# Moving entry 0's stores to ScalarE's queue, ending its projections four steps early, and telling the planner what entry 0 leaves open

## The chip, the cores and the metric

The kernel runs on one core of a Trainium2 chip. A core has five engines that work side by side and wait for each other through semaphores: TensorE (PE in the profile; its weight loads are PEld), VectorE (DVE), ScalarE (ACT), GpSimd (POOL) and SyncE (SP), which here only issues DMAs. Each engine takes its instructions in order; a DMA is issued by an engine's queue and then runs by itself on sixteen DMA engines. The metric is the device time of one execution in microseconds; three executions of the kernel before are known, and one more was profiled.

## The reference

The inputs are `x` of shape (8, 2048, 256) in float32 (eight entries of a batch, 2048 nodes, 256 features) and a 2048 x 2048 0/1 matrix `adj`. Two graph layers follow, each as a residual with a layer norm:

```
layer 0:  v = x W (8 heads of 32);  e_ij = leaky_relu(es_i + ed_j, 0.2) + beta*log(adj_ij + 1e-6), -inf where adj_ij = 0
          x1 = layernorm(x + concat_h(softmax_j(e) v) W_out^T)
layer 1:  e_ij = leaky_relu((x1 W1)_i . (x1 W2)_j, 0.2), -1e12 where adj_ij = 0
          out = layernorm(x1 + relu(softmax_j(e) (x1 W3)))
```

## The kernel before

Everything is float32. Entry 0's layer 0 comes first and alone. Then, for each entry b, layer 1 of entry b runs together with layer 0 of entry b + 1, so that eight stretches of some 300 us follow the first one.

**Layer 0** works in strips. The heads go in four pairs, the 2048 queries in two halves; that makes eight units per entry, with 16 key tiles each: 128 strips. For one strip a tile `mt` (128 keys x 1024 queries, the weighted adjacency, kept in DRAM as `mt_d`) is loaded, VectorE makes two tiles `s` from it (L439 in entry 0, L988 later), and TensorE multiplies them with the values (`val`, L475) and, for some or all strips, with the denominator weights (`den`, L475). In entry 0 every strip has `val` and `den`. From entry 1 on, eleven strips of a unit first get a scaling by ScalarE (L424), and GpSimd sums them (L996) in place of `den`; the last five are direct.

**Entry 0** is written as a loop of 64 steps of two strips. In its first 16 steps it also builds the tiles: `make_m` (L220) loads a block of `adj`, VectorE, ScalarE twice and VectorE again turn it into `m` (L226 to L229), and `make_mt` (L235) transposes `m`, copies it on ScalarE (L241) and stores it to `mt_d` (L242). Between steps it advances the generator `others` (L793), which projects the seven other entries: TensorE's `proj` (L299), ScalarE's copies `v` and `both` (L301, L303), a store of `v` to `v_d` (L824), and at the end of each entry `factors` (the softmax factors `re`, stored by L827) and `queries` (the row `est`, stored to `c_d` by L340). The generator yields 56 times, 1.75 times per two steps, and once more after the loop for the last entry's `queries`.

When a unit ends, `divide` turns its denominator into a factor: a store and reload of `dn` to a narrow tile `rc` (L504), a reciprocal on VectorE and its store to `rec_d` (L508, L509), a load of the broadcast `rb` (L518), and a multiplication `ht` by `rb` on VectorE (L523). With the last unit's multiplication the head outputs of entry 0 are complete, and the projection `y` (L1115) can start.

**Who sets the order.** In entry 0 only TensorE's order is fixed, to the order of the code; the other engines are ordered by the framework. From L847 on every engine follows a written order, which a planner at build time (`Sched`, L660) writes out: it has a list of tasks with costs, dependencies, an extra latency `late`, and slots for the buffers (9 of them in the ring for `s`, 4 for `mt`), and emits at each moment the task that can start first. TensorE chooses between "full" work (`y`, the transposes `tr`, the projections `h`, the scores `e`, `T`, `acc`) and strips: when a strip is ready, it goes first if the strips eaten so far are behind a goal line by more than a few,

```
S.goal = lambda w: NP * 2 * NT * (w + 28.0) / span      # w: us of full work so far, span = 303
```

Each engine's and SP's part of this order starts with what is emitted right after L847: the last `queries`, then the second part of the last `divide` (reciprocal and store to `rec_d`), and then the planner's tasks. Four planner tasks named `tinyd` (L885) carry the rest of that `divide`, the first of them the loads of `rb`; all the `y` wait for the last of them.

Of the kernel before, what the change touches and what calls it, by code (L numbers as in the profile page):

```python
# [18 lines left out]
P = 128  # L19
# [8 lines left out]
def kernel(  # L28
# [26 lines left out]
    nc = tc.nc  # L55
    B, N, D = x.shape
    H, _, DH = w_proj.shape
    NT = N // P
# [5 lines left out]
    NP = H // HP  # L64
    IG = BK // P
# [2 lines left out]
    J2 = NT // 2  # L68
    DIRECT = [[range(NT)] * NP] + [[(11, 12, 13, 14, 15)] * NP] * (B - 1)
    SLOTS = 9  # L70

    const = ctx.enter_context(tc.tile_pool(name="const", bufs=1))
    dram = ctx.enter_context(tc.tile_pool(name="dram", bufs=1, space=DRAM))
# [8 lines left out]
    def mm_tile(name):  # L82
        tag = banks[0]
        banks.append(banks.pop(0))
        return pacc.tile([P, BK], F32, tag=tag, name=name)
# [3 lines left out]
    def pair_tile(name):  # L89
        pairs.append(name)  # L90
        return pacc.tile([P, 2, BK], F32, tag=f"c{len(pairs) % 2}", name=name)

    homes = {"s": [f"s{i}" for i in range(SLOTS)], "h": [f"h{i}" for i in range(4)], "mt": [f"mt{i}" for i in range(4)],
             "row": [f"row{i}" for i in range(4)]}
# [15 lines left out]
    def leave(t):  # L110

        home, at, _ = home_of.pop(id(t))
        homes[home].append(at)
        return at
# [4 lines left out]
    def h_tile(name, shape, tag=None, dtype=F32):  # L119
        return home_tile("h", name, shape, dtype, tag)  # L120
# [54 lines left out]
    def later_weights():  # L175

        nc.sync.dma_start(w3s, w3.rearrange("(k p) d -> p k d", p=P))
        w1t, w2t = (chunk.tile([P, KC, D], F32, tag="pt", name=name, bufs=NB) for name in ("w1t", "w2t"))
        for w, dst in ((w_out, wot), (w1, w1t), (w2, w2t)):
            src = [row_tile("square") for _ in range(KC)]  # L180
            for o in range(KC):
                nc.sync.dma_start(src[o], w[ts(o, P), :])
            yield
            for kc in range(KC):
                t = mm_tile("sq_t")
                for o in range(KC):
                    nc.tensor.transpose(t[:, ts(o, P)], src[o][:, ts(kc, P)], ident)
                nc.scalar.copy(dst[:, kc, :], t[:, 0:D])
        yield
        for dc in range(KC):  # L190
            t = mm_tile("w12p")
            for kc in range(KC):
                nc.tensor.matmul(t[:, 0:D], w1t[:, kc, ts(dc, P)], w2t[:, kc, :], start=(kc == 0), stop=(kc == KC - 1))
            nc.scalar.copy(w12[:, dc, :], t[:, 0:D])
        yield


    mt_d = dram.tile([2 * J2, P, 2, HALF], F32, name="mt_d")
    pen_d = dram.tile([N, N], BF16, name="pen_d")
    c_d = dram.tile([B, H, N], F32, name="c_d")  # L200
    v_d = dram.tile([B, NP, P, NT, HP * DH], F32, name="v_d")
    re_d = dram.tile([B, P, 2, NT, H], F32, name="re_d")
# [3 lines left out]
    def load_x(b, g):  # L206

        xg = wide.tile([P, IG, D], F32, tag="pen", name="xg", bufs=1)
        nc.sync.dma_start(xg, x[b].rearrange("(t p) d -> p t d", p=P)[:, ts(g, IG), :])
        return xg  # L210

    def transpose_x(xg, dst):

        for kc in range(KC):
            t = mm_tile("tr")
            for k in range(IG):
                nc.tensor.transpose(t[:, ts(k, P)], xg[:, k, ts(kc, P)], ident)
            nc.scalar.copy(dst[kc], t)
# [13 lines left out]
    def mt_tile(tag=None):  # L232
        return home_tile("mt", "mt", (P, HALF), F32, tag)

    def make_mt(n, i, m):  # L235

        mt = mt_tile()
        t = pair_tile("mtp").rearrange("p a n -> p (a n)")
        for k in range(NT // 2):
            nc.tensor.transpose(t[:, ts(k, P)], m[:, k, ts(i, P)], ident)  # L240
        nc.scalar.copy(mt, t)  # L241
        nc.sync.dma_start(mt_d[n, :, i], mt)  # L242
        return mt

    def load_mt(n, i, tag=None):
# [4 lines left out]
    def row_tile(name, tag=None):  # L250
        return home_tile("row", name, (P, D), F32, tag)
# [14 lines left out]
    class Gat:  # L266


        def __init__(self, b):
            self.b = b  # L270
            self.ms, self.mts, self.v, self.mv = [], [], {}, None
# [62 lines left out]
        def queries(self):  # L334

            t = mm_tile("est")
            nc.tensor.transpose(t[:, 0:P], self.sums_c.rearrange("p h t -> p (h t)"), ident)
            est = row_tile("est")[:, 0:P]
            nc.scalar.activation(est, t[:, 0:P], AF.Exp, scale=1.0 - ALPHA)
            nc.sync.dma_start(c_d[self.b].rearrange("h (t p) -> (h t) p", p=P), est)  # L340

        def load(self, hp):
            self.v[hp] = chunk.tile([P, NT, HP * DH], F32, tag="v", name="v", bufs=2)
# [294 lines left out]
    class Task:  # L638
# [8 lines left out]
        def ready(self):  # L647
# [9 lines left out]
                t = max(t, at)  # L657
            return t

    class Sched:  # L660


# [130 lines left out]
    def others():  # L793

        order = gats[2:-2] + gats[1:2] + gats[-2:]
        groups = [(gat, g) for gat in order for g in range(NB)]
        xgs, xts, xtiles = [], [], []

        def load(n):
            if n < len(groups):  # L800
                xgs.append(load_x(groups[n][0].b, groups[n][1]))

        def turn(n):
            if n < len(groups):
                xt = h_tile("xt", (P, KC, BK))
                xtiles.append(xt)
                xts.append([xt[:, kc, :] for kc in range(KC)])
                transpose_x(xgs[n], xts[n])
                load(n + 1)

        load(0)
        yield
        turn(0)
        for n, (gat, g) in enumerate(groups):
            if g == 0:
                gat.begin()
            v = chunk.tile([P, NP, IG, HP * DH], F32, tag="v", name="v", bufs=2)
            for k in range(0, IG, 2):
                gat.rows_in(g * IG + k, xts[n], v[:, :, ds(k, 2), :])
                if k == 0:  # L820
                    turn(n + 1)
                else:
                    leave(xtiles[n])
                    nc.sync.dma_start(v_d[gat.b].rearrange("h p t f -> p h t f")[:, :, ts(g, IG), :], v)  # L824
                    if g == NB - 1:
                        gat.factors()
                        nc.sync.dma_start(re_d[gat.b], gat.re)  # L827
                    if g == 0 and n > 0:
                        groups[n - 1][0].queries()
                yield  # L830
        order[-1].queries()
        yield

    projections, weights = others(), later_weights()
    next(projections)
    count = (B - 1) * NT // 2
    for k in range(1, NP * NT + 1):
        g0.step(k - 1)
        if k % 2 == 0:
            for _ in range(k * count // (NP * NT) - (k - 2) * count // (NP * NT)):  # L840
                next(projections)
            if k > NT:
                next(weights, None)
# [1 line left out]


    ctx.enter_context(tc.manual_schedule(engines={e.engine for e in (nc.sync, nc.scalar, nc.vector, nc.gpsimd)}))  # L847
    next(projections)
    S = Sched()
    bank = Banks(["m0", "m1", "den"])  # L850
    for work in later:
        next(work)
# [10 lines left out]
    def pe(where, name, busy, emit, deps=(), hold=None, reader=None, easy=True, seam=False):  # L863
# [8 lines left out]
        if reader:  # L872
            queue, rbusy, remit, rdeps = reader
            r = Task(queue, rbusy, lambda: remit(box["t"]), [task] + list(rdeps), (), [hold])
            task.reader = r
            task.after = lambda: S.q[queue].append(r)
        task.box = box
        getattr(S, where).append(task)
        return task

    pending = []
    last = None
    for work in later:
        for _ in range(4):
            last = S.add("tinyd", 0.3, lambda work=work: next(work, None), [last], late=3.0)  # L885
    pending.append(last)
    later[:] = []

# [7 lines left out]
    def layer0(b):  # L896

        gat, E = gats[b], entries[b]
        E.mult, E.turned = {}, None
        E.re = S.add("v", 0.4, gat.load_factors, late=3.0) if b > 1 else None  # L900
        for hp in range(NP):
            if b > 1 or hp > 0:
                hold = Hold(v_s, NT * 2)
                load = S.add("v", 0.4, lambda hp=hp: gat.load(hp), takes=[hold], late=4.0)
                vs = S.add("vscale", 1.15, lambda hp=hp: gat.scale(hp), [load])
            else:
# [284 lines left out]
    def layer1(b):  # L1191
# [175 lines left out]
        def new(it):  # L1367
            R[it] = {"e": [], "T": [], "pts": [], "ph": [], "a": []}

        queries(0)  # L1370
        new(0)
        for c in range(NB):
            scores(0, c)
        soft(0)
        for it in range(NT):
            more = it + 1 < NT
            if more:
                new(it + 1)
            for c in range(NB):
                turn(it, c)  # L1380
                if more:
                    scores(it + 1, c)
            if more:
                soft(it + 1)
            for h in range(8):
                acc(it, h)
            if it + 2 < NT and (it + 2) % IG == 0:
                queries((it + 2) // IG)
            if it == NT - 3:
                E.near = R[it]["a"][-1]  # L1390
# [15 lines left out]
    for a in range(HP):  # L1406
        u.makes[NT - 1, a].after = lambda a=a: bank.give(u.makes[NT - 1, a].end, f"c{a}")
    span = 303.0
    S.goal = lambda w: NP * 2 * NT * (w + 28.0) / span
    S.run()  # L1410
# [1 line left out]
_INS = ['x', 'adj', 'L0_gnn_W', 'L0_gnn_a_src', 'L0_gnn_a_dst', 'L0_gnn_beta_tilde', 'L0_gnn_W_out',  # L1412
# [27 lines left out]
```

## Time and profile before

| | |
|---|---|
| median of 3 runs (lowest, highest) | 4111.2 us (4104.77, 4113.67) |
| the profiled execution's own time | 4113.88 us |
| its span | 4112.1 us |
| PE, DVE, ACT, POOL busy | 97%, 76%, 71%, 67% of the span |
| granted TensorE clock, mean | 0.993 |
| entry 0 (0 to 460 us): PE, DVE, ACT busy | 427.6, 380.7, 187.7 us |
| 460 to 480 us: PE busy | 3.3 of 20 us |
| 480 to 600 us: PE busy | 108.0 of 120 us |
| 900 to 3600 us: PE busy | 2644.6 of 2700 us |

The span is the profiled execution from its first to its last instruction. A busy time is the time in which an engine had an instruction in it; a matmul that waits for its input in the middle of a group counts as busy in part, so a stretch can be emptier than its PE figure. Windows of the trace give the same figures for any stretch, the list of waits says who ended an engine's idle time, and the chain of waits goes back from the last instruction of a stretch to what released each step.

### The profile page before, as it was taken

The numbers are of one execution on the slowest core, as the hardware profiler recorded it, in microseconds if no ns is written. First come the engines' busy times: TensorE is split into PE (matmuls) and PEld (weight loads), VectorE is DVE, ScalarE is ACT, GpSimd is POOL, SyncE is SP. The second block draws the span as 40 slices with busy tenths as digits, with TensorE's granted clock in tenths as the row PEclk, the third lists the DMA queues.
The fourth block names the chain that finished last, engine by engine and source line by source line (L and its number), as shares of the span: only waits on it lengthen the run. The fifth ranks groups of instructions, "written<-read, shape, count | busy, mean of one in ns | idle before, by whom it ended". The sixth has DMA issues, their size and how long they took to land.

```text
span 4112.1 us, 60541 instructions
## 1 busy us (share of the span) xinstructions
PE 3973.1 (97%) x22704; PEld 2157.4 (52%) x22704; DVE 3144.8 (76%) x3343; ACT 2927.6 (71%) x4164; POOL 2747.1 (67%) x1318
## 2 busy tenths in 40 slices
PE   8999899999999999999999999999999999999999
PEld 5444444555555555545555554555555554555666
DVE  7888678788877888888877888878877888786222
ACT  6522478887777778777877788778877887776554
POOL 0000279878787788888878898878878887885000
PEclk9999999999999999999999999999999999999999
DMA  8899767777656666666665676656665666654111
GB/s 274 287 293 308 249 207 242 230 242 260 200 187 199 215 198 207 200 204 220 208 209 185 198 229 209 213 183 223 224 199 185 215 229 207 191 196 131 63 47 41
DMA packets 346439, 843.65 MB, mean 205 GB/s; under 512 B 49696, under 2 KB 166432, under 8 KB 346144
## 3 DMA queue, kind: packets, MB, share of 16 engines
q1 hardware_dynamic: 346144, 839.77, 62.6%
q8 instruction: 178, 2.92, 0.3%
q14 instruction: 117, 0.96, 0.1%
HBM read 763.76 MB, written 75.37 MB: 204 GB/s over the span
## 4 chain that ended last, share of the span: by engine, by line
PE 59%; ACT 11%; DVE 7%; DMA 5%; issue 3%; POOL 3%; SPq 0%; DVEq 0%; ACTq 0%; POOLq 0%
PE e L1229 18%; PE acc L1324 14%; PE val L475 12%; ACT s L424 6%; DVE s L988 5%; PE den L475 5%; PE T L1304 4%; PE h L1178 3%; DMA mt<-mt_d 2%; POOL sums L996 2%; PE h L1204 2%; DVE p L1275 1%; ACT p L1236 1%; PE y L1115 1%; DMA rc<-dn 1%
## 5 line engine op out<-in xcount | busy, mean ns | idle before, releaser
L996 POOL TENSOR_TENSOR sums<-sums,s 128x1024 f32<-128x1024 f32 x1008 | 2366.8, 2389 | 17.6 <-DVE s L988 15.7
L988 DVE SCALAR_TENSOR_TENSOR s<-c,re,s 128x1024 f32<-128x1024 f32 x1232 | 1513.7, 1274 | 285.8 <-ACT s L424 245.7
L424 ACT ACTIVATE s<-mt,re 128x1024 f32<-128x1024 f32 x1232 | 1350.7, 1147 | 104.0 <-DMA mt<-mt_d 75.3
L475 PE MATMUL val<-s,v 128*32 128x512 f32 x8192 | 1014.8, 598 | 32.3 <-issue 14.6
L1229 PE MATMUL e<-x1t,h 128*128 128x512 f32 x2048 | 981.5, 604 | 24.0 <-ACT p L1236 18.2
L1324 PE MATMUL acc<-h,pts 128*128 128x256 f32 x4096 | 911.9, 381 | 0.7 <-ACT pts L1309 0.7
L1324 PEld LDWEIGHTS acc<-h,pts 128*128 128x128 f32 x4096 | 775.5, 190 | 177.1 <-issue 61.9
L988 DVE SCALAR_TENSOR_TENSOR s<-c,re,mt 128x1024 f32<-128x1024 f32 x560 | 679.3, 1275 | 44.1 <-POOL sums L996 18.5
L475 PEld LDWEIGHTS val<-s,v 128*32 128x32 f32 x8192 | 245.2, 110 | 613.9 <-issue 481.7
L1229 PEld LDWEIGHTS e<-x1t,h 128*128 128x128 f32 x2048 | 352.1, 191 | 378.1 <-issue 280.6
L1275 DVE CUSTOM_DVE_ANT_0 p<-p,pen 128x2048 f32<-128x2048 f32 x128 | 336.3, 2627 | 264.8 <-ACT p L1236 260.2
L1236 ACT ACTIVATE p<-e 128x512 f32<-128x512 f32 x512 | 304.7, 595 | 205.2 <-PE e L1229 198.2
L1276 POOL TENSOR_SCALAR neg<-neg 128x1 f32<-128x1 f32 x128 | 26.6, 208 | 615.9 <-DVE neg L1275 610.1
L475 PE MATMUL den<-s,re 128*32 128x512 f32 x3264 | 437.1, 593 | 0.0
L1281 ACT ACTIVATE p<-p,neg 128x2048 f32<-128x2048 f32 x128 | 256.1, 2001 | 223.4 <-POOL neg L1276 222.4
L1304 PEld LDWEIGHTS T<-ident,p 128*128 128x128 f32 x2048 | 250.1, 141 | 281.4 <-issue 174.4
L996 POOL TENSOR_TENSOR sums<-s 128x1024 f32<-128x1024 f32 x112 | 264.7, 2384 | 181.4 <-DVE s L988 181.3
L439 DVE SCALAR_TENSOR_TENSOR s<-c_in,re,mt 128x1024 f32<-128x1024 f32 x256 | 310.4, 1278 | 38.5 <-DMA mt<-mt_d 30.3
L1304 PE MATMUL T<-ident,p 128*128 128x128 f32 x2048 | 311.3, 276 | 24.3 <-ACT p L1281 13.8
L1309 ACT COPY pts<-T 128x512 f32<-128x512 f32 x512 | 296.6, 583 | 30.6 <-PE T L1304 29.3
L310 POOL PARTITION_ALL_REDUCE top<-top x8 | 7.4, 920 | 410.4 <-DVE top L309 410.4
L475 PEld LDWEIGHTS den<-s,re 128*32 128x32 f32 x3264 | 107.9, 110 | 240.9 <-issue 239.4
(99 smaller groups left out, 2476.2 us busy)
## 6 DMA issues: line engine op xcount, KB each, us to landing
mt<-mt_d SPq DMA_DIRECT2D x992, 512.0 KB
c_in<-c_d SPq DMA_DIRECT2D x64, 1024.0 KB
pen<-pen_d SPq DMA_DIRECT2D x112, 512.0 KB
xg<-in_x_dram SPq DMA_DIRECT2D x60, 512.0 KB
adj_t<-in_adj_dram SPq DMA_DIRECT2D x16, 1024.0 KB
mt_d<-mt SPq DMA_DIRECT2D x32, 512.0 KB
rb<-rec_d SPq DMA_DIRECT2D x128, 128.0 KB
adj_r<-in_adj_dram SPq DMA_DIRECT2D x32, 512.0 KB
```

What stands on the lines that cost most here:

```text
L424: nc.scalar.activation(self.s[jt][:, a], self.mt[jt], AF.Copy, scale=self.gat.re[:, 1, jt, h:h + 1])
L439: nc.vector.scalar_tensor_tensor(s[:, a], self.c[a], self.gat.re[:, 0, jt, h:h + 1], m, ALU.max, ALU.mult)
L475: nc.tensor.matmul(dst[ts(q, DH), :], weights[q % 2], s[:, q % 2, ts(q // 2, BK)], start=start, stop=stop)
L988: nc.vector.scalar_tensor_tensor(u.s[jt][:, a], u.c[a], gat.re[:, 0, jt, h:h + 1], m, ALU.max, ALU.mult)
L996: nc.gpsimd.tensor_tensor(u.sums[:, a], of[:, a], u.s[jt][:, a], ALU.add)
L1229: nc.tensor.matmul(t, box["h"][:, kc, ts(it % IG, P)], gat.x1t[:, kc, ts(c, BK)], start=(kc == 0), stop=(kc == KC - 1))
L1236: nc.scalar.activation(pbox["p"][:, ts(c, BK)], t, AF.Prelu, alpha=ALPHA)
L1275: nc.vector.tensor_tensor_reduce(p, p, r["pen"], 1.0, -FMAX, ALU.subtract, ALU.max, neg)
L1281: nc.scalar.activation(p, p, AF.Exp, bias=r["neg"], accum_out=den)
L1304: nc.tensor.transpose(t[:, ts(k, P)], pbox["p"][:, ts(c * IG + k, P)], ident)
L1309: nc.scalar.copy(pt, t)
L1324: nc.tensor.matmul(r["acc"], r["pts"][g][:, ts(k, P)], gat.h3[:, j, :], start=(j == 0), stop=(j == NT - 1))
```

## The change

The planner's and entry 0's orders change in five places.

1. Four DMA issues of entry 0 and its projections go from SP's queue to ScalarE's: the stores to `mt_d`, `c_d`, `v_d` and `re_d`. All of them store what ScalarE wrote.
2. The 56 yields of the projections are spread over 60 steps and not 64, and the last `queries` comes at step 60 and not after the loop, so it's no longer part of the written order.
3. The planner's clock for TensorE starts at 13.0 and not at 0.
4. The first `tinyd` becomes ready at 18.0 and not at 0, and each of the four has 2.0 and not 3.0 of latency.
5. The lead of 28 in the strips' goal grows with the work: 28 * min(1, (10 + w) / 303).

```diff
+    EARLY = 4
@@ make_mt
-        nc.sync.dma_start(mt_d[n, :, i], mt)
+        nc.scalar.dma_start(mt_d[n, :, i], mt)
@@ Gat.queries
-            nc.sync.dma_start(c_d[self.b].rearrange("h (t p) -> (h t) p", p=P), est)
+            nc.scalar.dma_start(c_d[self.b].rearrange("h (t p) -> (h t) p", p=P), est)
@@ new class
+    class Ready:
+        def __init__(self, end):
+            self.end, self.eng, self.late, self.name = end, None, 0.0, "ready"
@@ others
-                    nc.sync.dma_start(v_d[gat.b].rearrange("h p t f -> p h t f")[:, :, ts(g, IG), :], v)
+                    nc.scalar.dma_start(v_d[gat.b].rearrange("h p t f -> p h t f")[:, :, ts(g, IG), :], v)
                     if g == NB - 1:
                         gat.factors()
-                        nc.sync.dma_start(re_d[gat.b], gat.re)
+                        nc.scalar.dma_start(re_d[gat.b], gat.re)
@@ the loop of entry 0
-            for _ in range(k * count // (NP * NT) - (k - 2) * count // (NP * NT)):
+            for _ in range(min(count, k * count // (NP * NT - EARLY)) - min(count, (k - 2) * count // (NP * NT - EARLY))):
+                next(projections)
+            if k == NP * NT - EARLY:
                 next(projections)
@@ after the written order begins
-    next(projections)
     S = Sched()
+    S.pe = 13.0
@@ the planner's tasks
-    last = None
+    last = Ready(18.0)
     for work in later:
         for _ in range(4):
-            last = S.add("tinyd", 0.3, lambda work=work: next(work, None), [last], late=3.0)
+            last = S.add("tinyd", 0.3, lambda work=work: next(work, None), [last], late=2.0)
@@ the strips' goal
-    S.goal = lambda w: NP * 2 * NT * (w + 28.0) / span
+    S.goal = lambda w: NP * 2 * NT * (w + 28.0 * min(1.0, (10.0 + w) / span)) / span
```

## The prediction

> **What bounds the kernel now.** I read the page's forty slices first: TensorE is full from the fifth slice on, so time is lost only where it idles, and that is before about 900 us. The windows then price the places:
>
> ```profile
> 100.00:150.00 50.00, 42.31 (x290) 23.57 (x291) 45.84 (x39) 36.84 (x35) 1.24 (x1) 0.93 0.86 284
> 400.00:450.00 50.00, 50.00 (x380) 24.08 (x373) 44.54 (x41) 10.69 (x28) 3.70 (x2) 1.00 0.81 274
> 450.00:500.00 50.00, 31.14 (x171) 15.19 (x170) 18.92 (x25) 25.50 (x37) 13.99 (x8) 0.83 0.65 225
> ```
>
> Columns: stretch, length, busy PE, PEld, DVE, ACT, POOL, granted clock, DMA share, GB/s. Up to 150 us DVE is the full engine and PE idles 27.9 us in sum (start included); from 150 to 460 us PE is full; at the seam to the written order it loses 18.9 us of 50. From 500 to 900 us it idles 17.7 us more, from 900 on 1 us per 50.
>
> The chain of waits around the seam:
>
> ```profile
> 465.31 0.31 ACT re L316
> ...
> 466.27 0.38 SPq L340
> ...
> 466.75 1.46 DMA rec_d<-rc
> ...
> 469.14 0.37 SPq L1255
> ...
> 470.04 7.37 DMA mt<-mt_d
> 477.43 2.21 ACT s L424 x3
> 479.64 10.65 DMA mt<-mt_d
> ```
>
> Start, length, what. The last projection's factors hold SP's store of `est` (L340), behind it `rec_d`, then the `rb` loads, the `adj` rows, and only then entry 1's `mt`. The first strip runs at 480.0, after PE's last projection at 463.0. The VectorE timeline shows the reciprocal done at 462.2, so the `est` chain cost `rec_d` 4.5 us:
>
> ```profile
> 461.99 0.25 DVE L508 RECIPROCAL rc<-rc 128x16 f32<-128x16 f32 x1 [13.38 <-DMA rc<-dn]
> ```
>
> In the first stretch SP waits in line for ScalarE, and what is behind it comes late (SP's waits up to 620 us; then the timeline):
>
> ```profile
> SPq L242 <- ACT mt L241: 54.0, 30, 3.8
> SPq L824 <- ACT both L303: 38.0, 14, 11.0
> ```
>
> ```profile
> 132.51 7.62 SPq L224 DMA_DIRECT2D adj_t<-in_adj_dram  x2
> 137.43 2.28 DVE L229 SCALAR_TENSOR_TENSOR m<-adj_t,m 128x2048 f32<-128x2048 int32 x1
> 139.77 3.53 PE L240 MATMUL mtp<-ident,m 128*128 128x128 f32 x16 [6.21 <-DVE m L229]
> ```
>
> The `adj` load of 132.5 had its buffer free at 126.7, when an L229 ended; SP stood behind `v_d`, `re_d` and two `mt_d` stores. PE idled 6.2 us nearby.
>
> **What the Trainium skill says.** "DMA: Bandwidth & Descriptors", section "Issuing engines are not separate DMA queues": SP's and ScalarE's DMAs run on the same engines, and spreading them saves only the issue time. So part 1 gains no bandwidth, only SP's waiting; the trace has the DMA share at 0.81 to 0.93 in entry 0. Its section "Queues, rings and completion order": SP and ACT own one row of rings each, served in turn, so a store no longer stands behind SP's loads. "TensorE: Matmul & The Clock Gate", "What's actually happening": an idle PE falls to half clock; the trace agrees, 0.50 in 470 to 480 us.
>
> **The change part by part.** Each sum is against the profiled 4113.88 us (span 4112.1 and 1.8 around it), 2.7 above the median of 4111.2.
>
> *1, stores on ACT.* 32 `mt_d`, 28 `v_d`, 8 `c_d`, 7 `re_d`: 75 issues leave SP. An issue takes 0.32 to 0.46 us on SP; on ACT the trace has none. Below: nothing, if it overlaps ACT's pipeline; above: 0.45 us. I take 0.38, so 28 us of ACT. After 150 us that's hidden: ACT is busy 11 to 21 of 50 and PE full. Before, ACT is at 37 to 39 of 50 and gets about 42 issues, 16 us; behind each stand the Ln and Exp of the next `m` and, behind those, DVE's L229. I put +1.0 on the path (0 to +4). The gain: in 50 to 150 us DVE idles 5.8 us, of which some 3 come from the late L226 and L229; a free SP loads `adj` up to 5.9 us earlier. -3.0 (0 to -5, since DVE can't be fuller than full; the framework may also write another order, which could turn the sign: +2).
>
> *2, projections early.* By step 16, 14.9 yields have run in place of 14.0. One has 8 matmuls in 2.0 us and half the time 1.0 us of transposes, 2.5 us. It moves from where PE is full to where it idles: -2.4 (0 to -3). The rest moves within the full stretch: the two yields after the last strip (459.05 to 463.0) now come before it, so the last strip ends at about 463, not 459.1, and PE's total is unchanged. SP's written order loses `c_d`, but keeps `rec_d` at its head. After 463: `ht` copies and `dn` 1.0, `rc` 1.9, reciprocal 0.2: `rec_d` at 466.2 against 466.75. The wait for `est` is replaced by the wait for the last strip: -0.5 alone.
>
> *3 and 4, 13.0 and 18.0.* Following the planner's costs (for order, not time): `rb` was first on SP; now adj rows, four `mt`, `c_in`, `v`, two `x` and six more `mt` go first. Gain: `rec_d`'s wait and four `rb` issues, 467.19 to 469.04, leave the way, and 0.5 MB leaves the queue ahead: the first `mt` lands near 474 in place of 477.4, -3.4. Loss: TensorE's order was two strips, then `y`; I find eight strips, then `y`. The tenth `mt`, ahead of `rb`, waits for the scaling of strip 5. `mt` number 4 landed 12.9 us after the first, so near 487; two strips of scaling, 2.1 us each: `rb` issued at 491, landed near 495, multiplied by 497, strip 7 made by 499. `y` starts near 500, not 484.9. By then PE has done 8 strips of 0.86 us, 6.9; before, by 500, 6 strips and 5 `y` of 1.84, 14.4: +7.5 behind. Given back: from 485 to 557 PE stalled 12.3 us (2.0 and 1.2 at `y` and `tr`, strips stretched by 3.3 to DVE's pace, 3.7 and 2.1 at a reciprocal that waited 7.1 us for `rc`). After 500 the backlog of DMAs is gone and `y` to `h` can run on end; I leave 4.5 of it: -7.5. Sum 0 (-5 to +9).
>
> *5, the goal.* At the start it asks for 0.4 strips, not 11.8. From 557 to 600 PE idles 4.9 us in the windows, some 8 with stretched matmuls, at layer 1's first mask and exponential, with nothing made left to run. With strips held, up to seven made ones wait there, 0.86 us each, 6.0: I take -5, less 1 for buffers that they keep, -4 (-7 to +3). Later the goal is the old one; the rewritten order moves every entry by chance: their idle ran from 3.3 to 10.3 us per 300, so +-4.
>
> Sum: +1.0 - 3.0 - 2.4 - 0.5 + 0 - 4 = -8.9, so 4105.0 for a run like the profiled one, and by the median **4102**.
>
> **Rivals.**
> *No change (within 0.2%).* DVE or ACT gives back part 1, and the `y` loss is recovered but no more: about -3, 4108. For it: DVE is busy 94 of 100 us in 50 to 150; PE's total is the same. Against: PE idle in place.
> *Slower: the written order waits for a plan that came true late.* SP's first instruction still waits for the last strip, 16 us after the planner's zero at 450, while its plan has strips running. Then `y` waits for `rb` behind the `mt` loads. If `y` starts after 500 and the 7.5 us aren't given back, with a cold PE's 2 us and the next unit's `rc` wait again, the seam costs +12 to +16 against entry 0's -4: 4122. It decides once the loss from 463 us to the first `e` exceeds that of before (34 of the 94 us from 463 to 557: the rest is 8 `y`, 8 `tr`, 8 `h`, two first scores projections and some 23 strips) by about 13.
> *Much faster.* The framework gets entry 1's loads in before the last `rc`, while PE still has its 13 us of strips: the idle from 463 to 480 goes, 4088. Against: `rec_d` is first in SP's written order.
> *ScalarE's stores do nothing* is part of the second case: then only -3 is lost.
>
> **How the numbers follow.** A 0.2% bound, 8.2 us, is what a measurement can tell from no change: faster is below 4103.0, slower above 4119.4. The forecast has 0.44, no change 0.31, slower 0.18, much faster 0.07. So faster 0.51, same 0.31, slower 0.18. The forecast's own range is 4094 to 4108; to hold 8 in 10 it reaches up into the slower case and down into the much faster one: 4088 to 4120.
>
> **What would show it.** Right: `adj` loads issued as soon as L229 ends; PE over 43 busy in 100 to 150 us; the last strip followed by `rc`, `rec_d`, `adj` rows, `mt` with no `est`; first strip near 476; eight strips before the first `y` near 500; fewer PE gaps from 557 to 600. Wrong: longer gaps between ACT's Ln, Exp and copies in the first 150 us; a seam to the first `e` that takes 10 us more; `mt` loads before `rec_d`; or a steady stretch after 900 us that changes by more than 1 us per 300.

## The result, and the profile after

| | median, us (lowest, highest) | runs |
|---|---|---|
| before | 4110.47 (4104.77, 4113.67) | 6 |
| after | 4137.30 (4133.66, 4140.45) | 6 |

The ratio after to before is 1.0066, with a 95% interval of 1.0053 to 1.0079: slower by some 27 us. 4102 was predicted, and 4120 was the upper end of the range. The profiled execution of after took 4138.9 us, with a span of 4137.1, 25.0 more than before.

In after the code up to the new class stands one line further down, what follows the class some nine: `m`'s first pass on VectorE, which reads the `adj` block, is L227 (L226 before), its last pass, which reads the block once more and so frees its buffer, is L230 (L229), the strips' `s` of entry 0 are L440 (L439).

These windows of after answer to those of before (stretch, length, busy PE, PEld, DVE, ACT, POOL, granted clock, DMA share, GB/s):

```profile
100.00:150.00 50.00, 40.64 (x284) 23.35 (x277) 37.81 (x29) 30.25 (x35) 0.00 (x0) 0.90 0.75 256
400.00:450.00 50.00, 46.61 (x325) 23.65 (x321) 38.37 (x35) 12.04 (x30) 1.87 (x2) 0.93 0.93 304
450.00:500.00 50.00, 44.99 (x341) 19.42 (x337) 35.98 (x33) 10.48 (x24) 0.40 (x1) 0.97 0.59 186
500.00:550.00 50.00, 24.99 (x106) 5.63 (x99) 26.71 (x22) 27.02 (x27) 27.07 (x12) 0.70 0.76 262
```

The seam has moved from 450 to 500 us: entry 0 takes longer. From 100 to 150 us VectorE, which was the full engine before with 45.84, is busy for 37.81 and does 29 instructions in place of 39. TensorE, VectorE and ScalarE all do less, so they wait for something else. Entry 0's last matmul ends at 463.0 before and at 503.75 after. What follows takes 3649.1 us before and 3633.4 after. So **entry 0 lost 40.7 us, and all that comes later gained 15.7**.

In the first 230 us the waits of after (engine and line, releaser: us in total, times, longest) have VectorE's wait for the `adj` load at 35.1 us. It was 9.8 before. In both the first load of all is 7.6 to 7.9 us of that, so the rest grew from 1.9 us to 27.5.

```profile
DVE m L227 <- DMA adj_t<-in_adj_dram: 35.1, 10, 7.6
...
PE mtp L241 <- DVE m L230: 24.4, 7, 7.9
```

```profile
SPq L225 <- DVE m L230: 102.6, 13, 13.5
```

The second fence is SP's part of the same view: SP no longer stands in line for ScalarE (54.0 and 38.0 us before, up to 620 us), as predicted. It now stands at the next `adj` load and waits for VectorE's last pass to free the buffer. The chain of waits in after shows that as a loop (start, length, what):

```profile
79.13 2.21 DVE m L230
81.34 0.02 issue
81.36 8.21 DMA adj_t<-in_adj_dram
...
89.69 0.06 DVE m L227
...
93.31 2.21 DVE m L230
95.53 0.02 issue
95.54 5.49 DMA adj_t<-in_adj_dram
...
101.15 0.17 DVE m L227
```

A last pass frees a buffer, the load for it is issued within 0.03 us, and VectorE's next first pass is already waiting for it. From 60 to 200 us `adj_t` is 36.8% of the chain. Nothing here is issued late. The release is late, because VectorE's order is another one. `adj` has two buffers, so the last pass of block n frees the buffer for block n+2. These are the orders that the framework wrote for VectorE, for most blocks (F a last pass, R a first pass, s the pair of instructions that makes the two tiles of one strip):

```
before   F(n)  R(n+1)  s s  F(n+1)  R(n+2)  s s      from F(n) to R(n+2): R, s, s, F
after    F(n)  s  R(n+2)  s  F(n+1)  s  R(n+3)  s    from F(n) to R(n+2): s
```

Lines of VectorE's timeline show it, first of before, from F(9) to R(11), then of after, behind the F that the chain has at 79.13 us:

```profile
104.88 2.29 DVE L229 SCALAR_TENSOR_TENSOR m<-adj_t,m 128x2048 f32<-128x2048 int32 x1
107.17 1.23 DVE L226 TENSOR_SCALAR m<-adj_t 128x2048 f32<-128x2048 int32 x1
108.32 4.87 DVE L439 SCALAR_TENSOR_TENSOR s<-c_in,re,mt 128x1024 f32<-128x1024 f32 x4
...
115.05 2.29 DVE L229 SCALAR_TENSOR_TENSOR m<-adj_t,m 128x2048 f32<-128x2048 int32 x1 [0.62 <-ACT m L228]
117.25 1.22 DVE L226 TENSOR_SCALAR m<-adj_t 128x2048 f32<-128x2048 int32 x1
```

```profile
81.25 2.47 DVE L440 SCALAR_TENSOR_TENSOR s<-c_in,re,mt 128x1024 f32<-128x1024 f32 x2
89.69 1.23 DVE L227 TENSOR_SCALAR m<-adj_t 128x2048 f32<-128x2048 int32 x1 [5.97 <-DMA adj_t<-in_adj_dram]
```

By these orders before has some 8.4 us of other work between a release and the next use of the buffer (1.2 + 4.9 + 2.3). Counted block by block in its timeline, from the fourth block on, it is 6.1 to 13.2 us, with one exception of 2.5. After has 2.5 us for five of its last nine blocks and 4.9 for three. The load takes 5.5 to 8.2 us in the chain of after. It was not faster with the stores on SP: one of before took 6.2 us (issued at 90.03, landed by 96.23), one of e1_sp 9.15. Part 1 names no VectorE instruction; but only TensorE's order is fixed in entry 0, and the framework ordered VectorE anew around the moved stores.

At the seam the chain of after answers to that of before:

```profile
504.77 1.84 DMA rc<-dn
...
506.91 0.32 SPq L510
...
508.23 6.48 DMA mt<-mt_d
...
514.74 4.27 ACT s L425 x4
...
532.72 0.42 SPq L519
...
534.12 6.21 DMA rb<-rec_d
...
547.67 2.43 PE y L1124 x5
```

It goes in the order that the prediction gave: `rec_d`, `adj` rows, `mt`, strips, and only then `rb` (L519) and `y`.

### The profile page after: what moved, and what is told of

Read it like the earlier page. It is cut to its first block, busy times and chain, and to the rows that moved or that the text cites. A ratio compares the mean times of both kernels' runs of the same rounds, so it can differ in the third digit from the quotient of the medians.

```text
span 4137.1 us, 60541 instructions
## 1 busy us (share of the span) xinstructions
PE 3973.6 (96%) x22704; PEld 2163.0 (52%) x22704; DVE 3152.1 (76%) x3343; ACT 2929.0 (71%) x4164; POOL 2749.4 (66%) x1318
## 4 chain that ended last, share of the span: by engine, by line
PE 64%; ACT 11%; DVE 10%; DMA 8%; issue 4%; POOL 3%; SPq 0%; DVEq 0%; ACTq 0%; POOLq 0%
PE e L1238 18%; PE acc L1333 14%; PE val L476 14%; PE den L476 6%; ACT s L425 5%; DVE s L997 5%; PE T L1313 4%; DMA mt<-mt_d 3%; POOL sums L1005 2%; PE h L1187 2%; PE h L1213 2%; DVE s L440 2%; DVE p L1284 2%; DMA adj_t<-in_adj_dram 1%; PE proj L300 1%
## 5 line engine op out<-in xcount | busy, mean ns | idle before, releaser
L476 PE MATMUL val<-s,v 128*32 128x512 f32 x8192 | 1004.3, 600 | 38.1 <-DVE s L997 27.7
L440 DVE SCALAR_TENSOR_TENSOR s<-c_in,re,mt 128x1024 f32<-128x1024 f32 x256 | 311.4, 1278 | 43.1 <-DMA mt<-mt_d 24.5
```

The source lines that it names most:

```text
L440: nc.vector.scalar_tensor_tensor(s[:, a], self.c[a], self.gat.re[:, 0, jt, h:h + 1], m, ALU.max, ALU.mult)
L476: nc.tensor.matmul(dst[ts(q, DH), :], weights[q % 2], s[:, q % 2, ts(q // 2, BK)], start=start, stop=stop)
```

## The experiments

No experiment leaves out or changes any of the computation. "Before" is the median of before beside the same runs. First the change was taken apart.

**e2_act: part 1 alone.** Before, with these four lines:

```diff
-        nc.sync.dma_start(mt_d[n, :, i], mt)
+        nc.scalar.dma_start(mt_d[n, :, i], mt)
@@ and so for c_d, v_d, re_d
```

> The kernel before with part 1 alone (the four stores on ScalarE's queue). Order theory (the framework, which orders VectorE in entry 0, writes another order once these stores stand in ScalarE's queue: the first pass over the next adj block, L226, moves ahead of the last pass over the one before, L229, so that the load of the block after that starts later): the last strip of entry 0 ends near 500 us in place of 459, VectorE waits some 35 us for adj blocks up to 230 us, the time is about 4148. Issue theory (ScalarE's own work is held up by issuing the DMAs): the same time, but VectorE waits for ScalarE's Ln and Exp, not for adj. Projection theory (part 2 did it): 4110.

Measured 4146.69 against 4108.65, ratio 1.0101 (1.0078 to 1.0123). The whole loss and more is in part 1. VectorE has the order of after, its wait for `adj` is 38.0 us in 11, and `adj_t` is 38.1% of the chain from 60 to 200 us.

```profile
DVE m L226 <- DMA adj_t<-in_adj_dram: 38.0, 11, 8.0
```

That wait is 28.2 us more than before, and the last F begins 29.3 us later (189.65 us, before 160.31). The last strip ends 38.7 us later (497.8, before 459.1), so some 9 us more are lost behind the last F.

**e1_sp: parts 2 to 5, without part 1.**

```diff
@@ after
-        nc.scalar.dma_start(mt_d[n, :, i], mt)
+        nc.sync.dma_start(mt_d[n, :, i], mt)
@@ and so for c_d, v_d, re_d
```

> The changed kernel with part 1 undone (all four stores back on SP's queue; parts 2 to 5 stay). Order theory and issue theory: entry 0's last strip ends at 460 to 466 us, the time is 4137 less 41, about 4096. Projection theory: it stays near 4137.

Measured 4105.54 against 4108.65, ratio 0.9997 (0.9988 to 1.0006). With the stores back on SP, VectorE's order of F and R is again that of before, and that of the strips but for a few places; its wait for `adj` 12.6 us, and `adj_t` 6.5% of the chain from 60 to 200 us. It missed the expectation by some 9 us: its last strip ends at 471.2, not 463.

**e5_mt_sp: only `mt_d` back on SP.** `v_d`, `c_d` and `re_d`, 43 of the 75 issues, stay on ScalarE.

```diff
@@ after
-        nc.scalar.dma_start(mt_d[n, :, i], mt)
+        nc.sync.dma_start(mt_d[n, :, i], mt)
```

> The changed kernel with only the mt_d stores back on SP's queue; v_d, c_d and re_d stay on ScalarE's. VectorE's written order is then close to that of before. Order theory: entry 0's last strip ends below 472 us, the time is 4095 to 4105. Issue theory: 43 of the 75 issues stay on ScalarE, so about half of the loss stays: 4115 to 4120.

Measured 4106.64 against 4108.65, ratio 0.9996 (0.9982 to 1.0010): the same as with all four on SP, and just above what the order theory expected. So without the 32 `mt_d` issues the loss is gone, and the 43 others on ScalarE have no cost or gain that these intervals (some 6 us to either side) can tell. This agrees with the Trainium skill's "DMA: Bandwidth & Descriptors", section "Issuing engines are not separate DMA queues": all that another issuer saves is its issue time, here mostly 0.33 to 0.37 us each on ScalarE. But it didn't tell the two ways in which `mt_d` could cost apart: through VectorE's order, or by being issued between ScalarE's passes.

**e8_adj3: after, with a third `adj` buffer.** If the short way from release to use is the loss, a third buffer should lengthen it.

```diff
-        a = wide.tile([P, NT // 2, 2 * P], I32, tag="d", name="adj_t", bufs=2)
+        a = wide.tile([P, NT // 2, 2 * P], I32, tag="c" if n % 3 == 2 else "d", name="adj_t", bufs=1 if n % 3 == 2 else 2)
```

> The changed kernel with a third buffer for the blocks of adj (every third block goes to a buffer that entry 0 does not use yet); the four stores stay on ScalarE's queue, all 75 issues. Order theory: the loss is the time between the release of a block's buffer (L230) and the first use of what is loaded into it (L227), too short for a load of 6 to 8 us; with a third buffer VectorE's wait for adj up to 230 us falls from 35 us to under 15 and entry 0's last strip ends below 485 us, not at 503.8: about 4115. Issue theory: ScalarE still issues all, so the time stays above 4130.

Measured 4133.22 against 4109.87, ratio 1.0055 (1.0035 to 1.0075); the expectation of the order theory failed. The edit isn't clean: the framework wrote VectorE's order anew again, in places with two first passes in a row. Up to 230 us VectorE's wait for `adj` is 25.2 us (under 15 expected, 35.1 in after), and the last strip ends at 491.2 (below 485 expected); `adj_t` is still 22.8% of the chain from 60 to 200 us. Inconclusive.

**e13 and e14: VectorE's order written by hand, stores on SP and on ScalarE.** To hold the order fixed, `make_m` returns its last pass, `more_mt` runs it one step later, ahead of the next first pass, and VectorE joins TensorE in the fixed order.

```diff
@@ before (e13); with part 1 (e14)
-    ctx.enter_context(tc.manual_schedule(engines={nc.tensor.engine}))
+    ctx.enter_context(tc.manual_schedule(engines={nc.tensor.engine, nc.vector.engine}))
@@ make_m
-        return m
+        return m, lambda: nc.vector.scalar_tensor_tensor(m, a, 0.0, m, ALU.is_gt, ALU.mult)
@@ more_mt
+                if at < len(self.ends):
+                    self.ends[at]()
```

> Kernel before with VectorE's order in entry 0 written out by hand: last pass over block n, first pass over block n+1, then the four s tiles, step after step, as the framework mostly had it. The half of a pair; by itself 4105 to 4130, since a reciprocal or a factor that waits now holds VectorE in place. What counts is the difference to its partner with the stores on ScalarE.

> The same hand-written VectorE order with all four kinds of stores on ScalarE's queue; TensorE's and VectorE's orders are the same as its partner's, instruction for instruction. Order theory (the stores cost only through the order that the framework then writes for VectorE): within 5 us of the partner, last strip of entry 0 within 5 us of the partner's. Rival (issuing on ScalarE, or the order of ScalarE or SP, costs by itself): 25 to 40 us above the partner.

Measured 4165.02 and 4173.01 against 4109.4, ratios 1.0133 (1.0118 to 1.0148) and 1.0157 (1.0139 to 1.0175). By hand both are slow, well above the 4105 to 4130 expected: VectorE stands 10.5, 10.1 and 5.8 us at factors and values that the framework had placed later. The difference is 8.0 us, between what the two theories gave. As VectorE's stalls could hide a cost, a second pair was made.

**e16 and e17: the same, with those stalls taken away.** The fixed order begins only at the first step, and an entry's factors come one yield later.

```diff
@@ as e13 and e14, but
-    ctx.enter_context(tc.manual_schedule(engines={nc.tensor.engine, nc.vector.engine}))
+    ctx.enter_context(tc.manual_schedule(engines={nc.tensor.engine}))
@@ ahead of others()
+    ctx.enter_context(tc.manual_schedule(engines={nc.vector.engine}))
@@ others
+                if n > 0:
+                    groups[n - 1][0].factors()
+                    nc.sync.dma_start(re_d[groups[n - 1][0].b], groups[n - 1][0].re)
```

> Kernel before with VectorE's order written by hand only from the first step of entry 0 on (the stalls of the first hand-written pair at its start are gone), and each projected entry's factors moved one yield later, so that they don't hold VectorE. Its order is that of before in all but single places: 4104 to 4122.

> Its partner with all four kinds of stores on ScalarE, TensorE's and VectorE's orders the same. Order theory: the waits for the adjacency load stay near 10 us in 20 to 230 us and the time is at most 10 us above the partner (8 was what the first pair showed). Rival (issuing on ScalarE costs by itself where VectorE is full): 25 to 40 us above, with VectorE's waits on ScalarE's passes grown by as much.

Measured 4138.38 and 4147.23 against 4113.32, ratios 1.0064 (1.0049 to 1.0079) and 1.0079 (1.0062 to 1.0096). The partner with stores on SP is still 25 us slower than before, above its expectation. The difference is 8.9 us, as expected of the order theory (at most 10) and far from the 25 to 40 of its rival. VectorE's waits up to 230 us in e17, with all stores on ScalarE:

```profile
DVE m L229 <- ACT m L228: 21.4, 8, 4.0
DVE m L226 <- DMA adj_t<-in_adj_dram: 7.6, 1, 7.6
```

and SP's:

```profile
SPq L224 <- DVE m L229: 95.8, 12, 12.3
```

SP stands at the `adj` load about as long as in after (102.6), and VectorE doesn't wait for the load but once, for the first one: with R, s, s and F between release and use, the load has its time. So SP's wait by itself costs VectorE nothing, and the place of F is what counts.

What is left is 8.0 and 8.9 us by medians of four runs each; the single times of e16 and e17 just overlap (up to 4144.08, from 4142.32). The traces agree with it: the last strip ends 8.5 and 9.2 us later than in the partner (512.95 and 521.47; 485.44 and 494.65). Its cause stays open. In e17 VectorE waits longer than in e16 for ScalarE's last pass (21.4 us, 17.0 in e16), for the `mt` copies (6.2 from 38 to 230 us, 0.5 in e16) and for the reciprocal's `rc` (6.7, 0.8 in e16), and less for loads of `mt` and `adj` (9.1, 17.4 in e16). This need not be the issuing. The framework ordered ScalarE and SP anew here too, ScalarE idled for only 1.1 us right behind an `mt` or `est` copy of its own, and 4.4 us of the wait for copies go back to a load of `x`, for which TensorE waited 6.0 us (1.8 in e16).

So of the 38 us of e2_act some 9 come with the move even where VectorE's order is fixed, and the other 29 go with VectorE's order, as its waits for `adj` (28.2 us more) have it too. The 9 are carried over from kernels whose VectorE is less full than before's (39.45 of 50 us busy from 100 to 150 in e16). No run has the VectorE order of after with the stores on SP, which would have shown the order's cost directly.

**e3_early: part 2 alone.**

```diff
+    EARLY = 4
-            for _ in range(k * count // (NP * NT) - (k - 2) * count // (NP * NT)):
+            for _ in range(min(count, k * count // (NP * NT - EARLY)) - min(count, (k - 2) * count // (NP * NT - EARLY))):
+                next(projections)
+            if k == NP * NT - EARLY:
                 next(projections)
...
-    next(projections)
```

> Before with part 2 alone. By the prediction's step, -2.9: 4107. By what separates the runs with and without part 2 so far (last strip at 471 in place of 463): +5, 4114 to 4116.

Measured 4116.22 against 4109.4, ratio 1.0017 (1.0009 to 1.0026): part 2 costs 7 us. TensorE is busier in 50 to 150 us (90.2 of 100 us, before 88.7), but over the first 200 us only 0.8 us of that are left (172.3, before 171.5). Then TensorE's timeline has two new gaps in what was a full stretch:

```profile
417.70 0.48 PE L338 MATMUL est<-ident,cs 128*128 128x128 f32 x1 [6.06 <-ACT xt L219]
...
457.45 0.47 PE L338 MATMUL est<-ident,cs 128*128 128x128 f32 x1 [2.49 <-DVE cs L313]
457.85 1.94 PE L476 MATMUL val<-s,v 128*32 128x512 f32 x8
459.56 1.54 PE L476 MATMUL den<-s,re 128*32 128x512 f32 x8
```

`queries` is one transpose of 0.3 to 0.5 us, but it waits for the end of the factors (VectorE, GpSimd, VectorE), and TensorE keeps its order. Before, the last one stood behind the last strip, where TensorE had nothing to do. Now eight strips stand behind it, and the first matmuls after the gap take 1.94 and 1.54 us and not 1.04; the granted clock was 0.50 from 458 to 460 us. The Trainium skill ("TensorE: Matmul & The Clock Gate", "What's actually happening") has a PE at half clock after an idle window of some 3.4 us; this trace agrees on the half clock, but shows it after a gap of 2.49 us. After has the same wait, 4.10 us at 487.86. The gap of 6.06 us belongs to the sixth entry's `queries`: its all-reduce on GpSimd began at 415.01, 11.9 us after its input. Part 2 had moved this input up to 403.15 us (423.81 before), and in GpSimd's order a scaling of entry 1's values (L332) stood ahead, which ran from 407.61 to 408.34. The profile calls the last 6.7 us only "issue". In e1_sp the same happened, with 7.2 us behind the scaling; in before over 14 us lay between the two, and the all-reduce began 0.2 us after its input.

**e4_plan, e11_clock, e10_goal: parts 3 to 5, parts 3 and 4, part 5.** Each is before with these edits:

```diff
@@ parts 3 and 4
+    S.pe = 13.0
-    last = None
+    last = Ready(18.0)
-            ... [last], late=3.0)
+            ... [last], late=2.0)
@@ part 5
-    S.goal = lambda w: NP * 2 * NT * (w + 28.0) / span
+    S.goal = lambda w: NP * 2 * NT * (w + 28.0 * min(1.0, (10.0 + w) / span)) / span
```

> The kernel before with parts 3, 4 and 5 alone (13.0, 18.0, the goal). In the changed kernel what follows entry 0's last strip (503.8 us) took 3633.4 us, against 3649.1 before after its last projection (463.0). If the planner's parts bring these 15.8 us: 4095, with entry 0 as before and the first y some 40 us after the last projection. If they need the projections to end early: about 4110, no change. If the later y costs what the prediction's slower rival said: 4120.

> The kernel before with parts 3 and 4 alone (13.0 and 18.0, with the old goal). If the prediction is right that the eight strips ahead of y only cost what is given back later: 4105 to 4112. If the planner's clock brings the 7.5 us: 4100.

> The kernel before with part 5 alone (the strips' goal). Parts 3 to 5 together gave 4100.8, 7.5 us less than before. If the goal brings it, as the prediction has it: 4096 to 4102, and TensorE over 97 of 100 us busy from 600 to 700 us. If the clock and 18.0 bring it: 4108.

| | median | before | ratio (95%) |
|---|---|---|---|
| e4_plan, parts 3 to 5 | 4100.79 | 4108.65 | 0.9982 (0.9974 to 0.9990) |
| e11_clock, parts 3 and 4 | 4106.49 | 4109.87 | 0.9996 (0.9987 to 1.0005) |
| e10_goal, part 5 | 4094.38 | 4109.87 | 0.9964 (0.9949 to 0.9979) |

Part 5 alone gains 15 us, more than its range had, and slightly more than expected here; TensorE is busy for 96.7 of 100 us from 600 to 700 us (94.9 before), just short of the 97 expected. With parts 3 and 4 half of that gain is gone, so e4_plan has half of the 15.8 us that it was expected to bring. The groups of TensorE's instructions from 450 to 700 us (busy us, mean ns, idle before and releasers) show how, first of before, then of e10_goal:

```profile
L475 PE MATMUL val<-s,v 128*32 128x512 f32 x520 | 80.3, 626 | 27.9 <-issue 14.6 <-DVE s L988 12.3
L1229 PE MATMUL e<-x1t,h 128*128 128x512 f32 x80 | 41.2, 639 | 2.5 <-ACT p L1236 2.2 <-DVE z L1346 0.4
```

```profile
L475 PE MATMUL val<-s,v 128*32 128x512 f32 x520 | 69.0, 606 | 20.2 <-issue 15.3 <-DVE s L988 4.4
L1229 PE MATMUL e<-x1t,h 128*128 128x512 f32 x96 | 45.6, 603 | 0.5 <-ACT p L1236 0.3 <-ACT h L1209 0.2
```

As many `val` matmuls take 11.3 us less and wait 7.9 us less for `s`, and 16 more `e` matmuls got done in the same stretch. This fits the prediction's picture of strips held back, which run when their `s` is made and fill the gaps between the scores.

**e7_rec_later: `rec_d` not first in the written order.** Parts 2 to 5, stores on SP; the reciprocal and `rec_d` of the last `divide` are one more planner task.

```diff
@@ e1_sp
-    for work in later:
-        next(work)
-    last = Ready(18.0)
+    last = Ready(16.0)
-        for _ in range(4):
+        for _ in range(5):
```

> Parts 2 to 5 with the stores on SP, and the second half of the last divide (reciprocal and store to rec_d) no longer at the head of the written order but a planner task ready at 16.0. If SP's and VectorE's order blocks on it: entry 1's first mt loads are issued before the last strip ends, TensorE's 13.5 us without work after the last strip fall to under 4, and the time falls from 4105.5 by 8 to 14, to about 4094. If the later y sets the end of the seam anyway: 4105, no change.

Measured 4095.47 against 4109.87, ratio 0.9962 (0.9947 to 0.9977), as expected: 10 us better than e1_sp. The first `mt` loads are issued before the last strip ends (two at 457.93, the strip ends at 473.3), and TensorE's idle time after it falls from 13.55 us to 0.44. The prediction's claim that SP's first written instruction holds all that is behind it is right.

**e12_best: parts 3 to 5 with that, the projections spread as before, the last `queries` still in entry 0's own part.**

```diff
@@ e4_plan
+            if k == NP * NT:
+                next(projections)
-    next(projections)
@@ and the five tasks of e7_rec_later
```

> Before with parts 3, 4 and 5, stores on SP, projections spread as before; the last queries stay in entry 0's own part, and the last divide's reciprocal and rec_d are planner tasks (five tinyd, ready at 16) and not first in the written order. If the gain of the goal (15 us alone) and of the later rec_d (10 us) add up: 4084 to 4090. If they share one cause, the wait at the seam: about 4094, as each alone.

Measured 4089.82 (4087.55 to 4095.74), ratio 0.9953 (0.9937 to 0.9968): 20 us faster than before and some 46 faster than after. SP's timeline shows the four loads of `mt` issued while the last strips run, and `rec_d` 29 us later:

```profile
455.45 3.14 SPq L247 DMA_DIRECT2D mt<-mt_d  x4
...
484.81 0.38 SPq L509 DMA_DIRECT2D rec_d<-rc  x1
```

From 460 to 480 us TensorE is busy for 13.69 us in place of 3.31. That is the picture of the prediction's "much faster" rival, in part, and close to its 4088, reached by another edit and with part 5's gain in it. It lies at the edge of what was expected if the gains of e10 and e7 add up.

## Why the prediction was wrong

**Part 1, the gain of 3.0 and cost of 1.0 (0 to +4): the step that failed.** SP's waits for ScalarE are gone, and the `adj` loads are issued when the last pass ends, as predicted. But the step priced the move in the VectorE order that before has. The text names the risk, "the framework may also write another order, which could turn the sign: +2". That is what happened, and its size was some +29 by the split above, not +2: VectorE's waits for `adj` grew by 28.2 us in e2_act. Enough was known to size it from above: VectorE was full there, `adj` had two buffers, and the load was on record with a wait for L229; an order that leaves 2.4 us for a load of 6 to 8 can cost, as an estimate from these numbers, some 5 us a block, and with 16 blocks that is tens of us. The cost of +1.0 that comes without a new VectorE order is 8 to 9 by the two pairs, whatever makes it up; here the bound of +4 was too low as well.

The gain of 3.0 was misread too. From 50 to 150 us VectorE waited 2.1 us for `adj` and ScalarE's passes together, not some 3, and another 3.0 for an `mt` copy. The load of 132.51 held nobody: the R that reads its block follows at 139.63, right behind an F. A load that comes earlier had little to give.

**Part 2, -2.4 and -0.5.** Measured +7. The yields are whole numbers: 16 * 56 / 60 is 14.9, but the loop has made 14 by step 16, as many as before, and is one ahead only in steps 10 to 14. So nothing lasting moved out of the full stretch. The step "PE's total is unchanged" failed as well: the moved `queries` brought its wait with it. The prediction moved `est`'s store out of SP's order with care and didn't ask what TensorE, moved past the seam, would wait for there.

**Parts 3 and 4, the sum of 0 (-5 to +9).** Right: -3.4 alone, within what can be told from nothing. Step by step in after, counted from the last strip's end: the first `mt` landed after 11 us (11 predicted), eight strips ran before `y`, `rb` was issued after 29 (28 predicted) behind ten `mt`, and `y` began after 44 (37 predicted). The first `e` came 99 us after entry 0's last matmul, 94 in before, with 20 strips in between in both.

**Part 5, -4 (-7 to +3).** The mechanism fits, the size was too small: -15 alone, though some 8 of it is lost next to parts 3 and 4 (e4_plan -7.9). The predicted 5 us was the idle time of 557 to 600 us alone; up to 700 us the `val` group gave back 7.9 us in waits for `s` and 11.3 in matmuls that took less time.

**The steady stretch, +-4.** TensorE's busy time from 900 to 3600 us is 2646.9 us in after and 2644.6 before: no change, as said.

**The rivals.** The slower one (4122, the seam loses 12 to 16 us more) didn't happen: the seam lost 5, and what follows entry 0 gained 15.7. The outcome lay beyond it, in entry 0. "Against" the much faster one stood that `rec_d` is first in SP's order; e7 and e12 took that away and came near it.

The parts add up only roughly, by medians: -7.9 (parts 3 to 5), +4.8 by part 2 on top of them (e1_sp), +31.8 by part 1 on top of that.

## What to carry to other kernels

Where a framework orders the engines, moving an instruction to another queue is an edit of every engine's order: compare the written orders first, and price the new distance from each buffer's release to its next use against the duration of the load. A wait of an issuing queue for a free buffer need not cost anything, as long as the engine that frees it has other work until the load lands (e17). When a step is moved out of idle time, its own wait moves with it.

## What was not expected of the hardware

An issue of a store took mostly 0.33 to 0.37 us of ScalarE's queue, and the timeline has such an issue while a pass runs (in after at 75.52 us, under a pass from 75.39 to 77.40). The 43 issues without `mt_d` showed no cost (e5_mt_sp); with the 32 the time was 8 to 9 us longer although VectorE's order was fixed (e14, e17). What these 8 to 9 us are was not settled. Nor was it settled why, in two runs, an all-reduce on GpSimd began only 6.7 and 7.2 us after the scaling that stood ahead of it (e3_early, e1_sp).
